# Sums of a batch placed directly behind its last weighted values, the later tails in two parts, and the root table loaded first, in a perceiver block

## The chip, the core and the metric

The kernel runs on one core of a Trainium2 chip. A core has five engines that work through queues of their own, each in order: TensorE (PE in the profile; its weight loads are listed as PEld), VectorE (DVE), ScalarE (ACT), GpSimd (POOL) and SyncE (SP, which here only starts DMA transfers). They meet through semaphores. The metric is the device time of one execution in microseconds (us), from a median of several runs.

## The reference

A block of a perceiver: 8 batches of 64 queries of width 512 look at a context of 8 x 1601 x 512, then at themselves, and then go through a mixture of experts. All is in float32. Cut to what matters:

```python
def stablemax(x):
    s = jnp.where(x >= 0, x + 1.0, 1.0 / (1.0 - x))
    return s / jnp.sum(s, axis=-1, keepdims=True)

# cross attention: 16 heads of 32, over 1601 rows of context for each batch
q, k, v = layernorm(x) @ Wq.T + bq, ctx @ Wk.T + bk, ctx @ Wv.T + bv
attn = stablemax(q k^T / sqrt(32));  x = x + (attn @ v) @ Wo.T + bo
# causal attention among the 64 queries: 8 heads of 64 that share one k and one v
y = layernorm(x);  wei = softmax(causal(q k^T * 512**-0.5));  x = x + (wei @ v) @ Wp + bp
# feed-forward: the mean of 2 shared experts, and the best 2 of 8 experts for each row
y = layernorm(x);  gates = y @ rW + rb
x = x + mean_s(gelu(y @ sW1 + sb1) @ sW2 + sb2) + sum_top2(p * (gelu(y @ W1 + b1) @ W2 + b2))
```

The denominator of stablemax is a sum over all 1601 rows of context, so the division can be done once for each batch, on the result of `attn @ v`.

## The kernel before

**How the order is made.** Nearly all the work up to the routed experts is written down in a `Plan` (L50). `plan.add(length, fn)` lays units of TensorE work one behind the other and advances the planned clock by `length`; `plan.at(time, fn)` puts other work at a planned time. `emit` then calls all of it in order of planned time, and that is the order of the program. The planned times decide nothing but the order: a scheduler lays the calls into the queues of the five engines, and on the chip each engine goes on when its semaphores allow. PSUM has seven banks that all stages share (pool `ps_a`) and one for the weighted values (`ps_o`).

**Keys and values of the context.** Each batch has three sections of 512 rows of context and a tail of 65 (1601 = 3 x 512 + 65). Tails of four batches are done together: 64 rows of each as one half-size section, and the 65th rows of all batches as `odd_rows` (L507). `products` (its products are at L376) makes keys (`ps_k`) or values (`ps_v`) of a section from seven half-size products in the manner of Strassen, a *unit* each: VectorE joins two of them to what is there (L405), ACT copies the rest (helper at L87), and POOL makes the sums of the inputs (`context_part`, L365). Sums of weights are made by VectorE (L353). A unit of a section counts `PROD` in the plan, one of a tail half of it. Tails of batches 0 to 3 are made at the start, those of batches 4 to 7 (`tail_products(1)`, 7 units of keys and 7 of values with `last`, which writes the values to DRAM, L559) behind the last section of batch 4, since `NQB` is 4. `load_vt` (L570) reads them back for each batch.

**Cross attention.** Beside those products, in units of two 128-row tiles of context (the last unit of a batch is the tail alone): `score` (L631, `ps_s`), `convert` (ACT twice relu and once +1, VectorE's reciprocal at L649, POOL's additions at L650 and, for the denominators, L662) and `weigh` (L681, `ps_o`, summed over the batch). `when` holds the planned times of the scores and `weighed` those of the weighing. When a batch is through, `sums` (L702) multiplies its totals by ones into `ps_sum`; ACT copies them to `rec`, and VectorE takes the reciprocal (L709). `finish` (L716, L717; POOL) multiplies `o_sb` by `rec` and adds the bias: that is `ctT`.

**The chain.** For every two batches (a *tile* of 128 rows, four in all) `chain` lists steps with planned gaps: project (L738, `ps_wo`), factors and apply of the layernorm, turn (L324, transposes `pt`), keys (L775, `ps_akv`), queries (L788, `ps_aq`), scores, exps, flip (L833, `pt_s`), values (L844), output (L860, `ps_ap`), and the second layernorm with its transposes and gates (`factors`, `apply2`, `rows`, `gate`). A step of the last tile is 3.2 behind the one before or less; its TensorE neighbours are no longer sections but the first shared expert's hidden layer for two thirds of its size (`first_hidden`, L1099) and second layer (`first_second`, L1111), and then `SharedHalves`, which is built of the same seven units (`ps_hh`, `ps_hr`, also L376), its start (`xt`, L935) and its gelu (L947).

**The start.** The lines of constants: `eps_t`, `one_t` and `ones` are set by VectorE, and nine products of `ones` by `ones` into `ps_one` (L246) follow, whose result nobody reads. Then come the keys of the first section done plainly (`first_keys`, L465), `odd_rows`, `odd_turn` (L525: transposes the odd rows' keys; four ACT activations add the bias into `odd_k`), the first tails and the first layernorm (`first_rows`). `ln_rs`, the root of the variance, needs ACT's table for Sqrt.

The places that count for the order, as they stand before:

```python
weighed = [t + (n + 1.5) * step for t, n in zip(when, wide)]
weighed[-1] = when[-1] + 11.0
...
        done = weighed[last]
        more = 2.0 if b < B - 1 else 0.0
        plan.at(min(when[last] + 2.4 * step, done) + more, lambda b=b: sums(b))
        plan.at(done + 1.0 + 1.5 * more, lambda b=b: finish(b))
    ...
    time = done + 1.0
    for fn, wide in steps:
        time += gap * (wide if tt < NTT - 1 else min(wide, 1))
```

Of the kernel before, what the change touches and what calls it, by code (L numbers as in the profile page):

```python
# [10 lines left out]
F32 = mybir.dt.float32  # L11
U32 = mybir.dt.uint32
I32 = mybir.dt.int32
AF = mybir.ActivationFunctionType
ALU = mybir.AluOpType
# [3 lines left out]
P = 128  # L19
B, SQ, E = 8, 64, 512  # L20
SKV = 1601
NT = B * SQ
NTT = NT // P
NC = E // P
H1, HD1 = 16, 32
NG = H1 // 4
# [12 lines left out]
NSEC = SKV // SEC  # L39
# [56 lines left out]
def perceiver_kernel(  # L96
# [7 lines left out]
    nc = tc.nc  # L104

    act = InOrder(tc, nc.scalar)

    def pool(name, bufs, **kw):
        return ctx.enter_context(tc.tile_pool(name=name, bufs=bufs, **kw))

    const = pool("const", 1)
# [29 lines left out]
    def psa(name):  # L141
        return ps_a.tile([P, 512], F32, tag="a", name=name)
# [38 lines left out]
    NQB = B // 2  # L181
# [36 lines left out]
    bk_t = bias_cols(bk, NC, "bk_t")  # L218
# [17 lines left out]
    make_identity(nc, ident)  # L236
    eps_t = const.tile([P, 1], F32, name="eps_t")
    nc.vector.memset(eps_t, EPS)
    one_t = const.tile([P, 1], F32, name="one_t")
    nc.vector.memset(one_t, 1.0)  # L240
    ones = const.tile([P, P], F32, name="ones")
    nc.vector.memset(ones, 1.0)

    ps = psa("ps_one")
    for _ in range(9):
        nc.tensor.matmul(ps[:, :P], ones, ones, start=True, stop=True)  # L246

    qT = big.tile([P, NG, NT], F32, name="qT")
# [81 lines left out]
    plan = Plan()  # L330
# [3 lines left out]
    PROD = FULL / 2  # L334
# [155 lines left out]
    odd_k = const.tile([P, NG, B], F32, name="odd_k")  # L490
# [31 lines left out]
    def odd_turn():  # L522
        pt = psa("pt_odd")[:, : NG * B].rearrange("p (g b) -> p g b", g=NG)
        for g in range(NG):
            nc.tensor.transpose(  # L525
                pt[:, g, :], odd_rows.keys[0:B, g * P : (g + 1) * P], ident[0:B, 0:B]
            )
        for g in range(NG):
            act.activation(odd_k[:, g, :], pt[:, g, :], AF.Identity, bias=bk_t[:, g : g + 1])

    def tail_parts(h):
        p = tparts["t", h]
# [3 lines left out]
    def tail_products(h):  # L536
        def keys():
            kT = tlp.tile([P, NG, NQB, TAIL], F32, name="kTt", bufs=1)
            tails["odd", h] = kT[:, :, :, ROUND:TAIL].rearrange("p g b o -> p g (b o)")
            for k in range(NQB):  # L540
                tails[h * NQB + k, "k"] = kT[:, :, k, :]
            return kT

        def values():
            v = tails["v", h] = at4("vh").rearrange("p (k e) -> p k e", k=2)
            return v

        ku = products(
            ("t", h), True, dst=keys, hf=P,
            fit=lambda ps: ps.rearrange("p k (b s) -> p k b s", s=ROUND),  # L550
        )
        vu = products(("t", h), False, dst=values, hf=P)

        def last():
            vu[-1]()
            nc.gpsimd.tensor_copy(tails.pop(("odd", h)), odd_k[:, :, h * NQB : (h + 1) * NQB])
            v = tails.pop(("v", h))
            for k in range(NQB):
                nc.sync.dma_start(  # L559
                    out=vt_d[h * NQB + k, 0:ROUND, :],  # L560
                    in_=v[(k % 2) * ROUND : (k % 2 + 1) * ROUND, k // 2, :],
                )

        if h:
            return ku + vu[:-1] + [last]
        return ku[:2] + vu[:2] + ku[2:] + vu[2:-1] + [last]

    def load_vt(b):
# [127 lines left out]
    def sums(b):  # L696


        ps = psx("ps_sum")[:, : 4 * SQ]
        a = totals.pop(b)  # L700
        for j in range(4):
            nc.tensor.matmul(  # L702
                ps[32 * j : 32 * j + 32], ones[:, 0:32], a[:, j // 2, j % 2, :],
                start=True, stop=True, skip_group_check=True,
            )
        recs[b] = accp.tile([P, NG, SQ], F32, name="rec")

        act.copy(recs[b], ps.rearrange("p (g q) -> p g q", g=NG))
        sums.last = nc.vector.reciprocal(recs[b], recs[b])  # L709

    def finish(b):
        rec = recs.pop(b)
        if b % 2 == 0:
            ctT[b // 2] = sd("ctT")
        dst = cols(ctT[b // 2])[:, :, (b % 2) * SQ : (b % 2 + 1) * SQ]
        nc.gpsimd.tensor_mul(rec, accs.pop(b), rec)  # L716
        nc.gpsimd.tensor_tensor(  # L717
            dst, rec, bv_t.rearrange("p (g o) -> p g o", o=1).to_broadcast([P, NG, SQ]), ALU.add,
        )
# [404 lines left out]
    for i, (b, k) in enumerate(secs):  # L1124
        if i == 0:
            plan.add(4 * FULL, first_keys)
            there[i] = plan.now


            def early():  # L1130
                tail_parts(0)
                wkp.update(weight_parts(wk, "sk"))
                wvp.update(weight_parts(wv, "sv"))
                early.done = weight_parts.last
                weigh_bq()

            def sums_q():
                with tc.issue_after(Norm.last.ins):
                    wqp.update(weight_parts(wq, "sq"))

            plan.at(0.05, early)
            plan.add(2.0, odd_rows)
            for k, u in enumerate(tail_products(0)):
                if k == 2:
                    plan.add(0.3, odd_turn)
                plan.add(PROD / 2, u)
            for tt in range(NTT):
                plan.add(0.5, lambda tt=tt: first_rows(tt, early.done))
            plan.at(plan.now, sums_q)
            for n in range(4):  # L1150
                plan.at(plan.now + 0.01 * n, lambda n=n: context_part("q", n))
            tparts[0] = right_parts(cxs[0])
            values0 = products(0, False)
            for u in values0[:2]:
                plan.add(PROD, u)
            for u in products("q", True, wqp, qT, Q_SCALE, bqs_t):
                plan.add(PROD, u)
            asked = plan.now
            for n in range(4):
                plan.at(asked - 9.0 + 1.5 * n, lambda n=n: context_part(0, n))  # L1160
            for u in values0[2:]:
                plan.add(PROD, u)
            for tt in range(NTT):
                plan.at(plan.now + 4.0 * tt, lambda tt=tt: add_bo(tt))
            plan.add(0.0, act.bind)
        else:
            for u in products(i, True):
                plan.add(PROD, u)
            there[i] = plan.now
            for u in products(i, False):  # L1170
                plan.add(PROD, u)

        last = len(plan.units)
        if i + 1 < len(secs):
            start = plan.now - 14 * PROD
            if i == 0:
                plan.at(0.1, lambda: load_cx(1))
                for n in range(4):
                    plan.at(plan.now - 8.0 + 2.0 * n, lambda n=n: context_part(1, n))
            else:  # L1180
                plan.at(start + 0.1, lambda i=i: load_cx(i + 1))
                for n in range(4):
                    plan.at(plan.now - (6.5 - 1.5 * n) * PROD, lambda i=i, n=n: context_part(i + 1, n))
        if k == NSEC - 1:
            if b == NQB:
                plan.at(plan.now - 30.0, lambda: load_tails(1))
                plan.at(plan.now - 15.0, lambda: tail_parts(1))
                for u in tail_products(1):
                    plan.add(PROD / 2, u)
    end = plan.now  # L1190
    step = (end - 14.0) / len(tiles_in)
    units = [(b, u) for b in range(B) for u in range(len(UNITS))]
    nu = len(UNITS)
# [7 lines left out]
    when = [max(lag + n * step, asked + 1.0 + 0.8 * n * step) for n in place]  # L1201


    wide = [len(UNITS[u]) for _, u in units]
    weighed = [t + (n + 1.5) * step for t, n in zip(when, wide)]
    weighed[-1] = when[-1] + 11.0

    pairs = [0 < u < nu - 1 and u % 2 == 1 for _, u in units]
    for u, second in enumerate(pairs):
# [16 lines left out]
    for tt in range(NTT):  # L1226
        gap = 5.0 if tt < NTT - 1 else 3.2
        for bb in range(2):
            b = 2 * tt + bb
            last = (b + 1) * nu - 1  # L1230
            done = weighed[last]

            more = 2.0 if b < B - 1 else 0.0
            plan.at(min(when[last] + 2.4 * step, done) + more, lambda b=b: sums(b))
            plan.at(done + 1.0 + 1.5 * more, lambda b=b: finish(b))
        pre, steps = chain(tt)
        for fn in pre:
            plan.at(done - 10.0, fn)
        time = done + 1.0
        for fn, wide in steps:  # L1240

            time += gap * (wide if tt < NTT - 1 else min(wide, 1))
            if fn in asks and tt < NTT - 1:

                time = min(t for t in when if t >= time - 8.0) + 6.0
            plan.at(time, fn)
# [560 lines left out]
```

## Time and profile before

| what | value |
|---|---|
| median of 3 runs | 1356.39 us (1356.39 to 1356.93) |
| the profiled execution, its own time | 1357.59 us |
| its span, first to last instruction | 1355.9 us |
| mean granted TensorE clock | 0.998 |

Busy time of the engines by stage, in us, from the profile's windows:

| stage (us of the span) | PE | DVE | ACT | POOL | DMA share |
|---|---|---|---|---|---|
| 0 to 30: first keys, odd rows, first tails | 27.8 | 10.1 | 11.0 | 12.9 | 0.84 |
| 30 to 460: cross attention, first half | 428.7 | 387.4 | 279.5 | 375.8 | 0.18 |
| 460 to 880: cross attention, second half | 417.7 | 387.9 | 268.0 | 341.9 | 0.23 |
| 880 to 960: the last tile's chain | 77.4 | 62.5 | 32.3 | 3.3 | 0.53 |
| 960 to 1000: shared experts | 39.5 | 31.1 | 11.3 | 10.8 | 0.66 |
| 1000 to 1356: shared and routed experts | 349.1 | 91.9 | 72.4 | 19.7 | 0.61 |

A span is the time from the first to the last instruction of the profiled execution; its own time is a little longer. Busy time says how full an engine is, not whether anything waits for it. In the timelines, a line is a run of equal instructions with the start of the first, the time that they cover and their number; what stands in brackets is idle time in front of it and what ended it. L numbers are lines of the kernel before.

### The profile page before, as it was taken

What the parts mean: (1) busy time and instruction counts of PE and PEld (TensorE: products, weight loads), DVE (VectorE), ACT (ScalarE), POOL (GpSimd) and SP (SyncE); (2) the same over time, 40 slices, a digit from 0 to 9 for tenths busy, and PEclk for the clock granted to TensorE, in tenths of its full rate; (3) what the DMA queues carried; (4) which work ended last, traced back from release to release, by engine and by line L of the source; (5) the groups of instructions that cost most, each with busy time, mean ns of one, the idle gap of its engine ahead of it and who ended that gap; (6) DMA issues with size and microseconds to landing.
All of it is one profiled execution on the core that took longest, in us unless ns stands there. A gap on an engine that the chain in (4) does not pass through costs nothing.

```text
span 1355.9 us, 37790 instructions
## 1 busy us (share of the span) xinstructions
PE 1340.1 (99%) x16590; PEld 1121.9 (83%) x16590; DVE 971.0 (72%) x868; ACT 674.6 (50%) x1432; POOL 764.3 (56%) x686
## 2 busy tenths in 40 slices
PE   9999999999999999999999999999999999999997
PEld 6888888888788888878888877588898999977786
DVE  3499999998999997999998999887876200010314
ACT  4466666665666665766666667335222211122230
POOL 3789899888978986988889877600200000000020
PEclk9999999999999999999999999999999999999999
DMA  7211111122402122112113114436645936788721
GB/s 212 79 41 33 37 33 64 37 79 65 157 2 72 49 75 82 47 33 64 41 46 101 65 33 164 141 126 241 220 170 173 340 129 255 266 308 325 273 89 33
DMA packets 88280, 162.76 MB, mean 120 GB/s; under 512 B 13494, under 2 KB 15062, under 8 KB 88112
## 3 DMA queue, kind: packets, MB, share of 16 engines
q1 hardware_dynamic: 81232, 142.70, 31.1%
q0 software_dynamic: 4512, 13.92, 2.9%
q10 hardware_dynamic: 2368, 3.69, 0.9%
q8 instruction: 132, 2.16, 0.7%
q14 instruction: 36, 0.29, 0.1%
HBM read 148.50 MB, written 11.78 MB: 118 GB/s over the span
## 4 chain that ended last, share of the span: by engine, by line
PE 93%; DVE 3%; ACT 2%; POOL 1%; issue 1%; DVEq 0%; POOLq 0%; ACTq 0%
PE ps_k L376 22%; PE ps_v L376 21%; PE ps_h L1640 9%; PE ps_hh L376 7%; PE ps_hr L376 6%; PE ps_s L631 5%; PE y L1552 4%; PE y L1561 4%; PE ps_o L681 3%; PE ps_h L1099 2%; DVE neg L649 1%; PE y L1111 1%; PE ps_aq L788 1%; PE ps_k L465 1%; PE ps_wo L738 1%; PE ps_ap L860 1%
## 5 line engine op out<-in xcount | busy, mean ns | idle before, releaser
L649 DVE RECIPROCAL neg<-neg 128x512 f32<-128x512 f32 (+1 forms) x224 | 686.4, 3095 | 49.9 <-ACT neg L87 48.0
L650 POOL TENSOR_TENSOR at<-at,neg 128x512 f32<-128x512 f32 (+1 forms) x224 | 269.0, 1207 | 94.3 <-DVE neg L649 80.4
L662 POOL TENSOR_TENSOR tot<-tot,at 128x512 f32<-128x512 f32 (+1 forms) x176 | 224.9, 1278 | 13.1
L87 ACT ACTIVATE neg<-neg,one_t 128x512 f32<-128x512 f32 (+1 forms) x224 | 157.7, 704 | 0.0
L87 ACT ACTIVATE neg<-ps_s 128x512 f32<-128x512 f32 (+1 forms) x224 | 127.9, 571 | 56.9 <-PE ps_s L631 50.0
L1640 PEld LDWEIGHTS ps_h<-xgT,w1t 128*128 128x128 f32 x896 | 123.0, 191 | 27.8 <-issue 26.1
L87 ACT ACTIVATE at<-ps_s 128x512 f32<-128x512 f32 (+1 forms) x224 | 128.5, 573 | 23.5 <-PE ps_o L681 23.5
L1645 ACT ACTIVATE hT<-ps_h,b1e 128x128 f32<-128x128 f32 (+3 forms) x112 | 42.7, 381 | 194.8 <-PE ps_h L1640 194.8
L376 PE MATMUL ps_v<-sv,tx 128*128 128x256 f32 x576 | 132.5, 382 | 0.0
L1640 PE MATMUL ps_h<-xgT,w1t 128*128 128x128 f32 (+3 forms) x896 | 129.2, 287 | 0.0
L1543 POOL DMA_DIRECT2D ys_d<-yo x10 | 5.4, 544 | 219.6 <-DVE yo L1542 219.6
L376 PE MATMUL ps_k<-tx,sk 128*128 128x256 f32 x552 | 128.5, 384 | 0.6 <-DVE kT L405 0.6
L376 PEld LDWEIGHTS ps_v<-sv,tx 128*128 128x128 f32 x576 | 107.7, 190 | 17.6 <-issue 1.9
L376 PEld LDWEIGHTS ps_k<-tx,sk 128*128 128x128 f32 x552 | 102.7, 190 | 16.4 <-DVE kT L405 0.7
L87 ACT COPY v<-ps_v 128x512 f32<-128x512 f32 x96 | 56.6, 589 | 78.0 <-PE ps_v L376 77.9
L1534 DVE COPY xgT<-pt_x 128x512 f32<-128x512 f32 (+3 forms) x12 | 6.8, 593 | 119.4 <-PE pt_x L1533 119.4
L87 ACT ACTIVATE kT<-ps_k,bk_t 128x256 f32<-128x256 f32 (+1 forms) x142 | 60.9, 482 | 61.4 <-PE ps_k L376 54.9
L376 PE MATMUL ps_v<-wv,cx 128*128 128x256 f32 x384 | 89.4, 382 | 0.0
L376 PE MATMUL ps_k<-cx,wk 128*128 128x256 f32 x368 | 86.5, 383 | 0.0
L631 PEld LDWEIGHTS ps_s<-qT,kT 32*64 32x64 f32 x6144 | 70.4, 130 | 16.6 <-issue 14.4
L376 PEld LDWEIGHTS ps_v<-wv,cx 128*128 128x128 f32 x384 | 71.8, 190 | 10.8 <-issue 0.4
L631 PE MATMUL ps_s<-qT,kT 32*64 32x64 f32 x6144 | 77.4, 231 | 0.4 <-DVE v L405 0.4
(303 smaller groups left out, 2242.3 us busy)
## 6 DMA issues: line engine op xcount, KB each, us to landing
w1t<-in_W_dram SPq DMA_DIRECT2D x32, 1024.0 KB, 11.0
w2t<-in_W_dram SPq DMA_DIRECT2D x32, 1024.0 KB, 9.7
cx<-in_ctxT_dram SPq DMA_DIRECT2D x23, 1024.0 KB, 5.3
w1t<-in_sW_dram SPq DMA_DIRECT2D x14, 1024.0 KB, 6.3
w2t<-in_sW_dram SPq DMA_DIRECT2D x14, 1024.0 KB, 5.6
wo<-in_woT_dram SPq DMA_DIRECT2D x4, 1024.0 KB, 7.3
awq<-in_aWq_dram SPq DMA_DIRECT2D x4, 1024.0 KB, 7.2
awp<-in_aWp_dram SPq DMA_DIRECT2D x4, 1024.0 KB
```

Of the source, the lines that this page charges most:

```text
L87: ins = getattr(self.engine, name)(*args, **kw)
L376: nc.tensor.matmul(ps[:, k, :], l[:, c, k * P : (k + 1) * P], r[:, c, :], start=first and k == 0 and c == 0, stop=last and c == 1, skip_gr ...
L631: nc.tensor.matmul(ps[j][h, k, g, :], kT[rows, g, h], qT[rows, g, b * SQ : (b + 1) * SQ], start=True, stop=True, skip_group_check=True,)
L649: nc.vector.reciprocal(neg, neg)
L650: nc.gpsimd.tensor_add(pos, pos, neg)
L662: nc.gpsimd.tensor_add(tot, tot, at[:, :, i])
L681: nc.tensor.matmul(accs[b][32 * j : 32 * j + 32, g, :], v[:w, (4 * g + j) * 32 : (4 * g + j + 1) * 32], at[j // 2][:w, j % 2, k, g, :], st ...
L1099: nc.tensor.matmul(ps[:, :N0], w0[0, q][:, c, r * P : (r + 1) * P], shared_x["x"][:, c, :N0], start=c == 0, stop=c == NC - 1,)
L1552: nc.tensor.matmul(self.y[k], hT[:, s : s + w], w2t, start=first, stop=last)
L1561: nc.tensor.matmul(y[d // 2][:, d % 2, :], w2t[:, d * P : (d + 1) * P], hT[:, : self.n], start=first and d % 2 == 0, stop=last, skip_group ...
L1640: nc.tensor.matmul(ph[:, : blk.n], w1t[:, c, f : f + P], blk.x[:, c, :], start=c == 0, stop=c == NC - 1,)
L1645: nc.scalar.activation(hT[:, : blk.n], ph[:, : blk.n], AF.Gelu, bias=blk.bias(hc))
```

## The change

Six edits, in four groups.

1. **The start.** A Sqrt activation of `eps_t` into a tile that nobody reads is put right behind `eps_t`, so that ACT's first table is that of the root. Seven products of ones instead of nine. In `odd_turn` one VectorE addition with the bias broadcast takes the place of four ACT activations.
2. **The sums.** For the tail unit of every batch but the last, `weighed` grows by 2.0; `sums` is planned at that same time instead of up to 2.0 behind the weighing, and `finish` 2.0 behind it (before, 4.0 behind the old time of weighing). The chains of tiles 0 to 2 count from `done` and so are planned 2.0 later.
3. **The later tails.** `tail_products(1)` returns keys and values apart. The keys stay behind the last section of batch 4; the values come behind the keys of section 15, the first of batch 5.
4. **The last tile.** Its first step, project, is planned 4.8 instead of 3.2 behind `done + 1.0`, and all its other steps move with it.

```diff
     nc.vector.memset(eps_t, EPS)
+
+    root_t = const.tile([P, 1], F32, name="root_t")
+    nc.scalar.activation(root_t, eps_t, AF.Sqrt)
...
-    for _ in range(9):
+    for _ in range(7):
         nc.tensor.matmul(ps[:, :P], ones, ones, start=True, stop=True)
...
-        for g in range(NG):
-            act.activation(odd_k[:, g, :], pt[:, g, :], AF.Identity, bias=bk_t[:, g : g + 1])
+        nc.vector.tensor_tensor(
+            odd_k, pt, bk_t.rearrange("p (g o) -> p g o", o=1).to_broadcast([P, NG, B]), ALU.add
+        )
...
         if h:
-            return ku + vu[:-1] + [last]
+            return ku, vu[:-1] + [last]
...
             there[i] = plan.now
+            if i == (NQB + 1) * NSEC:
+
+                for u in later_values:
+                    plan.add(PROD / 2, u)
             for u in products(i, False):
                 plan.add(PROD, u)
...
-                for u in tail_products(1):
+                later_keys, later_values = tail_products(1)
+                for u in later_keys:
                     plan.add(PROD / 2, u)
...
+    for u, (b, v) in enumerate(units):
+        if v == nu - 1 and b < B - 1:
+            weighed[u] += 2.0
...
-            more = 2.0 if b < B - 1 else 0.0
-            plan.at(min(when[last] + 2.4 * step, done) + more, lambda b=b: sums(b))
-            plan.at(done + 1.0 + 1.5 * more, lambda b=b: finish(b))
+            plan.at(done if b < B - 1 else min(when[last] + 2.4 * step, done), lambda b=b: sums(b))
+            plan.at(done + (2.0 if b < B - 1 else 1.0), lambda b=b: finish(b))
...
-            time += gap * (wide if tt < NTT - 1 else min(wide, 1))
+            time += gap * (wide if tt < NTT - 1 else 1.5 if fn is steps[0][0] else min(wide, 1))
```

## The prediction

> **What bounds the kernel.** I read part 1 of the page first (busy time by engine), then part 4 (the chain that ended last).
>
> ```profile
> PE 1340.1 (99%) x16590; PEld 1121.9 (83%) x16590; DVE 971.0 (72%) x868; ACT 674.6 (50%) x1432; POOL 764.3 (56%) x686
> PE 93%; DVE 3%; ACT 2%; POOL 1%; issue 1%; DVEq 0%; POOLq 0%; ACTq 0%
> ```
>
> PE is busy for 1340.1 of 1355.9 us and makes 93% of the chain. No edit here removes products that matter, so only two things can be gained: PE's idle time, and the time that busy PE loses where one kind of product follows another. Next the list of PE's waits, which names nearly all the first.
>
> ```profile
> PE ps_akv L775 <- DVE kTt L405: 1.7, 1, 1.7
> PE ps_wo L738 <- POOL ctT L717: 1.6, 1, 1.6
> ...
> PE ps_k L376 <- ACT kTt L87: 0.9, 1, 0.9
> ...
> PE pt L324 <- ACT xn L87: 0.5, 1, 0.5
> PE pt_s L833 <- DVE s_a L827: 0.5, 1, 0.5
> ```
>
> Columns: waiting product, what released it, us in all, times, longest. Each occurs once, so each has a place: 517.9, 884.3, 29.3, 940.9 and 920.3 us. For the second kind, the timeline of PE at the end of batch 0 (start, duration, with records two to a product):
>
> ```profile
> 158.40 0.65 PE L681 MATMUL ps_o<-at,vt 65*32 65x64 f32 x32
> 158.98 1.99 PE L376 MATMUL ps_k<-tx,sk 128*128 128x256 f32 x8
> 160.91 0.64 PE L702 MATMUL ps_sum<-tot,ones 128*32 128x256 f32 x8
> 161.48 1.99 PE L376 MATMUL ps_k<-tx,sk 128*128 128x256 f32 x8
> 163.40 1.59 PE L631 MATMUL ps_s<-qT,kT 32*64 32x64 f32 x128
> ```
>
> Starts matter, not durations. A unit of eight full-array records between two groups of narrow products takes 1.93 us (158.98 to 160.91). Sixteen in a row take 3.45 us in the chain of waits (63.97), so eight take 1.73. Entering and leaving narrow products costs 0.20 us each time. The narrow side pays too: ps_o of the tail lasts 0.58 us before a full product (158.40 to 158.98), but 0.47 before ps_sum in batch 3 (464.50 to 464.97).
>
> **1. Seven products of ones, the root table first, odd_k on VectorE.** Two products are four records of 0.213 us, 0.85 us. PE would then start the keys at 4.46 us; their first chunk has landed at 4.14, the second at 4.70, the third (8.66) is wanted after 9.1, so no transfer is in the way. But the trace's records of ps_k come 0.43 us apart up to 7.01 us and 0.216 after. If that moment stays, the 0.85 us are filled with real products at half speed: 0.43 us gained. The Trainium skill, "TensorE: Matmul & The Clock Gate", Part 1, speaks against shortening a warm-up: about 3.4 us of sustained activity release the clock, by windows that run freely. PE is busy from 1.30 either way, so a free window puts the change at the same 7.0 us (0.43 gained). A clock moved by its phase could cost or give some tenths. I use the row.
>
> The next wait is at 29.3 us: ACT's copy of kTt stands behind a table load of 1.28 us and four odd_k of 0.73 us together. Both go: the first load moves to the start, where ACT is idle till 10.4, and the one at 25.76 disappears; VectorE gets one small addition (priced like ln_rs there, 0.16). "ScalarE: Activation LUTs", What ACT_TABLE_LOAD costs, gives 1.28 us plus a drain of 1.38 us for a switch, 2.66 in all; here ln_rs starts at 27.05, right behind the load from 25.76, so the row's 1.28 holds. Row: 1.28 + 0.73 could cover the 0.93 us wait fully; with the rule even more so. Neither decides, since the new order puts two xn before kTt and these need VectorE: its fourth BN statistics ends at 26.15 (its x tile landed at 25.4, and the queue in front of it is unchanged), then kTt's join 0.41, reciprocals and ln_nb 0.5, then on ACT two xn 1.5 and two kTt 0.6: 29.05, where PE restarts at 29.35 now. Gain for all of part 1: **0.3 us**, between 0 and 0.43 + 0.93 = 1.4. The order of issue on ACT changes too: wv now waits for the landing at 8.66 instead of starting its issue at 4.54. Its queue is filled by wk until 9.1, so it loses about 1 us there; it landed at 18.1 and PE wants it at 19.6. No cost, 0.4 us if that cover fails.
>
> **2. Sums behind the last weighted values.** In the built order, batches 0 to 6 now run tail ps_o, ps_sum, ps_s without anything between. Before, batches 0, 1 and 2 had a full unit in the first gap (in 2 the tail was split once more), and all seven one in the second. Merging ps_o with ps_sum saves 0.20 + 0.11 = 0.31, three times; ps_sum with ps_s 0.20 + about 0.06 (unseen: ps_sum before a full product takes 0.55 to 0.57, two passes of 256 columns at least 0.43, so 0 to 0.13), seven times; the split 0.31. That is 0.93 + 1.82 + 0.31 = 3.06. Lost elsewhere: two pt_s no longer beside ps_o (0.39), two akv no longer beside scores (0.65), akv of the last tile cut in two (0.3); won: aq beside ps_o (0.3). Net seven entries fewer of 111, **2.0 us**, between 1.4 (entries alone) and 2.5. The sums keep their place in time, since the tail values move to them by up to two units; ACT's waits on at come from the products before the tail, so it doesn't wait longer, and finish stays at four units of plan time behind the old weighing. SP's order around these places is the same.
>
> **3. The later tails in two parts.** akv waits for its PSUM bank until VectorE has joined kTt. VectorE's timeline:
>
> ```profile
> 511.02 6.55 DVE L649 RECIPROCAL neg<-neg 128x512 f32<-128x512 f32 x2
> 517.49 0.36 DVE L405 TENSOR_TENSOR kTt<-ps_k,kTt 128x256 f32<-128x256 f32 x1
> ```
>
> The join stands behind two reciprocals until 517.85. After the change PE has two more tail units (1.9 us) between the scores' end at 516.1 and the first product that needs this bank, a key unit of section 15: it comes at 518.0, when the bank is free. akv's own bank then is one that ACT frees. Gain **1.7 us**, between 1.2 (PE comes 0.5 earlier relative to VectorE) and 1.9. What moves: seven value units, with two VectorE joins (0.42 each), four ACT copies, one POOL addition, and on SP four vt_d stores from 535.4 to about 548. SP now issues section 17's load before them; section 18's follows at 562, and the first vt reader comes at 573.9 while the reloaded vt lands near 553. Hidden by some 12 us; past that, each us costs one.
>
> **4. The last tile's project later.** Its wait of 1.64 us (1.8 with the turn) goes, as four ps_hh units (3.6 us) now precede it. But three of those need the sums of weights behind rec on VectorE:
>
> ```profile
> 880.38 1.75 DVE L709 RECIPROCAL rec<-rec 128x256 f32<-128x256 f32 x1 [1.67 <-ACT rec L87]
> 882.05 1.75 DVE L353 TENSOR_TENSOR sw<-w1t 128x512 f32<-128x512 f32 x2
> 883.73 1.09 DVE L353 TENSOR_TENSOR sw<-sw,w1t 128x512 f32<-128x512 f32 x1
> ```
>
> PE ends y at 882.5 and the first unit at 883.4; the next needs the sum that ends at 884.8 (1.35 us of waiting), the third a copy of its bank by ACT (0.45). So 1.8 us are waited again, and ps_wo starts at 888.05. Then ACT, in order:
>
> ```profile
> 890.24 1.28 ACT L87 ACT_TABLE_LOAD   x1
> 891.88 0.29 ACT L87 ACTIVATE ln_rs<-ln_mv,eps_t 128x1 f32<-128x1 f32 x1 [0.36 <-DVE ln_mv L304]
> 892.19 1.28 ACT L947 ACT_TABLE_LOAD   x1
> 893.49 1.28 ACT L947 ACTIVATE hq<-hq,b_t 128x128 f32<-128x128 f32 x4
> ```
>
> In the new order one hq copy for the second half stands behind these four lines. They start at 895.5 there (behind a copy at 895.1), 4.1 us together, so the copy ends at 899.95, and PE, which wants its bank at 898.6, waits 1.3; xnT_a comes 0.6 late for akv as well. Against that, the waits at pt_s and pt (0.6 each with the turn) go, since 7.9 and 8.4 us of products lie in the chains that needed 7.5 and 8.5. Net: 1.8 - 1.8 - 1.9 + 1.2 = **0.7 us lost**, between 1.5 lost and 2.9 gained.
>
> **Sum.** 0.3 + 2.0 + 1.7 - 0.7 = 3.3 us. The profiled execution took 1357.59 us for a span of 1355.9, so it would take 1354.3; against the median of 1356.39 that is **1353.1 us**. A lead of PE survives as VectorE, though 92% busy from 440 to 640, idles repeatedly for PE's scores and so follows.
>
> **The rivals.**
> - The end stage gains: scheduling hides the weights' sums, all three waits there go (1.8 + 0.6 + 0.6 = 3.0). For: each is listed once and now has products before it. Against: VectorE's queue behind rec. 0.3 + 2.0 + 1.7 + 2.9 = 6.9: 1349.5 us. Chance 0.25.
> - VectorE takes the lead back: from 540 on it gets two joins more where it is full (38.55 of 40 us in 560 to 600), the akv wait returns at the next bank, and half of part 2 goes. 0.3 + 1.0 - 0.7 = 0.6: 1355.8 us. For: the three small waits on VectorE from 607 to 664. Against: nine us of its idle time in 520 to 540. Chance 0.22.
> - Slower: ACT decides the last tile. If tables and gelus come once more before something PE needs (oT before ps_ap, 925 to 935), one more such pass of 4.1 us is on the path, and the loss of part 4 is 4.8: 1357.2 us. It decides once the slack I count there, 1.9 us between oT and ps_ap, is used up. Chance 0.08.
> - My forecast as it stands has 0.45, with its own range 1351.8 to 1354.4.
>
> **Numbers.** A change under 0.2% (2.7 us) can't be told from none. Faster than 1353.7: three quarters of 0.45 and all of the first rival, 0.59; within: the rest of the forecast, the second rival and most of the third, 0.35; slower, 0.06. The range for 8 in 10, 1349.3 to 1356.5, reaches from the first rival to past the second.
>
> **What would show it.** Right: no wait at akv of the second tile; tail ps_o, ps_sum and ps_s at consecutive starts with 0.47 and about 0.5 us; PE's restart near 29; a wait of 1.3 us at ps_hh on sw, just before ps_wo, and one on ACT's hq copy near 898. Wrong: the end stage without those waits, or new waits on VectorE between 540 and 670.

## The result, and the profile after

| | before | after |
|---|---|---|
| median of 18 runs each, side by side | 1357.01 us (1355.57 to 1358.77) | 1358.16 us (1356.84 to 1364.07) |
| ratio | | 1.0015 (95% interval 1.0009 to 1.0021) |
| the profiled execution, its own time | 1357.59 us | 1357.48 us |
| its span | 1355.9 us | 1355.9 us |

The ratio is estimated from all runs and puts the change at 0.15% slower, 2.0 us (1.2 to 2.9); the two medians alone are 1.15 us apart. The forecast was 3.3 us faster. Nine of the eighteen runs after lie from 1356.84 to 1357.83 us, the profiled one among them, and nine from 1358.49 up: what those lose, this profile cannot show. The two profiles have the same span; that is chance, and the last part of this section says why.

From the page of the kernel after, busy time by engine and the chain that ended last:

```profile
PE 1337.4 (99%) x16586; PEld 1121.1 (83%) x16586; DVE 971.9 (72%) x869; ACT 674.6 (50%) x1428; POOL 764.1 (56%) x686
PE 91%; DVE 4%; ACT 2%; POOL 1%; issue 1%; DVEq 0%; ACTq 0%; POOLq 0%
```

TensorE is 2.7 us less busy, so the joined groups and the missing products of ones do save work (0.97 us of it is the clock's, see below); it is idle for 2.7 us more. The list of its waits says where (columns as in the prediction):

```profile
PE ps_s L635 <- issue: 2.4, 2, 1.4
PE ps_hr L379 <- DVE res L1067: 2.0, 2, 1.5
PE ps_hh L379 <- ACT hq L973: 1.8, 2, 1.3
PE ps_hh L379 <- DVE sw L356: 1.4, 1, 1.4
PE ps_one L249 <- DVE ones L245: 1.3, 1, 1.3
PE ps_k L379 <- DVE kT L408: 0.6, 1, 0.6
PE ps_k L379 <- DVE v L408: 0.5, 1, 0.5
```

The waits at akv, ps_wo, kTt, pt_s and pt that headed the list before are gone or down to 0.2 us. Five new ones stand in their place: the first four lines and the last, at 563 us. The first has no releaser at all: "issue" in the middle of a group of scores.

**Lead by place.** I compared the start of the same group in both traces. TensorE leads the kernel before by 1.40 us at the odd rows (20 us), 2.69 at the first scores (55), 4.07 from 366 to 449, 2.85 at 485, 4.28 at 663, 2.50 at 679 and 2.07 at 863. The stage from the last ps_sum to ps_c then takes 77.85 us instead of 74.24, so 3.6 us are lost, and the one from ps_c to the first pt_x 59.30 instead of 60.82, so 1.5 come back.

**Two things in that profile are not the change's.** The clock record begins at 5.04 us, against 6.99 before; 1.95 us at half speed are 0.97 us of the lead of 1.40, and the remaining 0.43 are the forecast's figure for the two products. The first full-speed record moves from execution to execution: 4.20 to 6.98 us in eleven further profiles (and 10.95 in one whose start was slowed). And the stage from ps_c to pt_x took 59.3 to 61.2 us over all profiles, 59.3 also in one without the last tile's part (e2), 61.0 in one with it (e7). Take both away, and the profile after is 2.5 us longer than before, near the 2.0 us of the ratio.

### The profile page after: what moved, and what is told of

It reads as the page before. It is cut to its first block, busy times and chain, and to the rows that moved or that the text cites. A ratio compares the mean times of both kernels' runs of the same rounds, so it can differ in the third digit from the quotient of the medians.

```text
span 1355.9 us, 37771 instructions
## 1 busy us (share of the span) xinstructions
PE 1337.4 (99%) x16586; PEld 1121.1 (83%) x16586; DVE 971.9 (72%) x869; ACT 674.6 (50%) x1428; POOL 764.1 (56%) x686
## 4 chain that ended last, share of the span: by engine, by line
PE 91%; DVE 4%; ACT 2%; POOL 1%; issue 1%; DVEq 0%; ACTq 0%; POOLq 0%
PE ps_v L379 21%; PE ps_k L379 20%; PE ps_h L1653 9%; PE ps_hr L379 7%; PE ps_hh L379 7%; PE ps_s L635 5%; PE y L1565 4%; PE y L1574 4%; PE ps_o L685 3%; DVE neg L653 3%; PE ps_h L1103 2%; PE y L1115 1%; PE ps_aq L792 1%; PE ps_k L468 1%; PE ps_ap L864 1%
## 5 line engine op out<-in xcount | busy, mean ns | idle before, releaser
L635 PE MATMUL ps_s<-qT,kT 32*64 32x64 f32 x6144 | 78.3, 232 | 3.0 <-issue 2.4
```

Of the source, the lines that this page charges most:

```text
L635: nc.tensor.matmul(ps[j][h, k, g, :], kT[rows, g, h], qT[rows, g, b * SQ : (b + 1) * SQ], start=True, stop=True, skip_group_check=True,)
```

## The experiments

Twelve kernels ran. "Before" in each is the kernel before, run beside it.

### The four parts alone

```diff
 e1_start: part 1 of the change alone      e3_tails: part 3 alone
 e2_sums: part 2 alone                     e4_last_tile: part 4 alone
```

> The kernel before with the start alone changed (root table first, seven products of ones, odd_k on VectorE). In the profile after, TensorE's lead over the kernel before is 1.40 us at the odd rows and 2.69 us at the first scores, so by the reading that each part keeps its own gain, this one is 2.7 us faster (-0.20%). By the rival reading, that a point late in the kernel (near 993 us, where both profiles stand at the same time) is set by another engine, leads are given back there and this is within 1 us of before. The forecast had said 0.3 us.

Measured: 1355.61 us against 1356.70, ratio 0.9997 (0.9988 to 1.0006). Eight of the twelve runs lie from 1354.3 to 1355.8, four from 1358.5 to 1360.2. The profiled one is of the four. Its clock record begins at 6.97 us, as before, so its leads are the part's own: 0.45 us at the odd rows, 1.74 at the first scores, 1.71 at 655. Then -1.59 at 679: in 20 us it loses 3.3 us, in a place that the edit doesn't touch. TensorE's windows there, from the profile of e1 (busy time and records of each engine, then the granted clock, DMA share and GB/s):

```profile
662.33:665.74 3.41, 1.81 (x103) 1.58 (x86) 2.84 (x2) 0.87 (x2) 3.33 (x3) 1.00 0.12 41
665.74:669.15 3.41, 3.41 (x32) 2.34 (x34) 0.44 (x1) 0.00 (x0) 3.33 (x5) 0.50 0.02 5
669.15:672.56 3.41, 3.41 (x125) 3.11 (x115) 1.56 (x2) 2.61 (x5) 2.02 (x3) 1.00 0.02 5
```

TensorE stands for 1.60 us inside its scores ("issue" again), and the granted clock is 0.50 in the next 3.41 us, which costs another 1.7. The fall comes 658.77 us after the clock's first record, 193 times 3.413 us, and the other six falls in these profiles lie at whole multiples too: a fixed grid of windows whose phase differs by execution.

> The kernel before with the sums alone moved. Changes between narrow and full products fall by some seven, worth 1.4 to 2.0 us. Theory of instruction pages: TensorE's instructions come in pages of 256, a page is there 3.3 us after its forerunner is entered, and narrow groups that lie side by side (336 instructions in 2.1 us) use up a page before the next is there; then stalls of up to 1.1 us stand inside ps_s or ps_o at instruction counts that leave the same rest (193) when divided by 256, and the gain shrinks to about 0.5 us, -0.5 to +1 us in all with a wo load that now falls into a dense stretch (1.7 us). Rival: the moved sums cost nothing and the part gains its 2.0 us.

Measured: 1355.17 us, ratio 0.9990 (0.9981 to 0.9999), 1.4 us faster. In its profile the lead grows by 0.10, 0.53 and 0.75 us at the ends of batches 0 to 2 (0.2 is lost between, near 326 us), falls by 1.5 in batch 3 (a stall of 1.45 us from start to start in the scores behind ps_sum, "issue", at TensorE instruction 14273), and is 0.76 us larger at 863 us than at 55. A new wait of 0.50 us stands at 551, of scores for VectorE's s_a. The wait at akv is absent here.

> The kernel before with the later tails alone split in two. The wait of 1.7 us at akv goes: 1.7 us faster if nothing takes its place, as forecast; within 0.5 us of before if VectorE sets the pace from 520 to 670 us and a new wait of the same size stands at a later join.

Measured: 1357.62 us, ratio 1.0006 (0.9997 to 1.0015). The lead is 0.10 us at 55 and 0.16 at 863: nothing gained. From the list of waits of e3:

```profile
PE ps_akv L775 <- DVE kTt L405: 1.6, 1, 1.6
```

The wait that this part was to remove is still there. It goes with part 2, whose chains are planned 2.0 later: in e2 two more tail units and half of a third stand between the scores and akv. And e3 has the new wait at ps_k for VectorE's join of v (0.48 us, at 567), as have all five profiles with part 3 and none of the nine without.

> The kernel before with the last tile's project alone planned 4.8 instead of 3.2 behind. Forecast: 0.7 us slower (ps_hh waits 1.4 and 0.5 for weights' sums and 1.3 for ACT, pt_s and pt no longer wait). From the profile after, where two waits on VectorE's res additions (1.5 and 0.5 us) come on top and 1.5 us of waits from 976 to 985 us go: 2.1 us slower. If the loss after 880 us came from the earlier arrival of the other parts instead, 0.7 us or less.

Measured: 1360.34 us, ratio 1.0030 (1.0018 to 1.0041): 4.1 us slower. The stage from the last ps_sum to ps_c takes 77.84 us, as after (77.85), and 74.23 to 74.25 in all nine profiles with project at 3.2. So the part costs 3.6 us, and nothing of it is due to the other parts.

### The change without the last tile's part

```diff
-            time += gap * (wide if tt < NTT - 1 else 1.5 if fn is steps[0][0] else min(wide, 1))
+            time += gap * (wide if tt < NTT - 1 else min(wide, 1))
```

> The changed kernel without its last part: project of the last tile at 3.2 again. The last tile alone had cost 2.3 us in its profile (lead 0.70 at 863 us, -1.62 at 1014) and 2.1 us in the profile of the changed kernel. If the parts add up, this is 2.2 us faster than the changed kernel: about 1355.5 to 1356, 0.5 to 1 us faster than before. Rival: TensorE's arrival near 968 us decides nothing, since waits of 1.5 us from 976 to 985 us come back, and it is within 1 us of the changed kernel.

Measured: 1356.63 us against 1357.26, ratio 0.9996 (0.9987 to 1.0004); the stage is back at 74.24 us. The sign agrees with the sum of the parts, the interval leaves the size open.

### TensorE's instruction pages

The fourteen profiles of this study hold 21 "issue" stalls of 0.1 us or more inside narrow groups from 30 to 900 us. Idle time is meant; from start to start it is 0.2 us more. All 21 stand at TensorE instruction numbers that leave the same rest, 193, when divided by 256 (all that TensorE's queue executes counted from 0: products, weight loads and some 200 others, nearly all for semaphores). The trace lists a packet of 16 KB on an instruction queue for every 256 such instructions, and TensorE goes on 1.29 to 1.47 us after the end of the latest one (the stalls of before and after). The one at 465 us, from the timeline of TensorE after:

```profile
462.39 0.65 PE L685 MATMUL ps_o<-at,vt 65*32 65x64 f32 x32
462.86 0.62 PE L706 MATMUL ps_sum<-tot,ones 128*32 128x256 f32 x8
463.41 1.58 PE L635 MATMUL ps_s<-qT,kT 32*64 32x64 f32 x126
465.92 0.27 PE L635 MATMUL ps_s<-qT,kT 32*64 32x64 f32 x2 [0.94 <-issue]
466.12 1.13 PE L379 MATMUL ps_v<-sv,tx 128*128 128x256 f32 x4
```

The three groups hold 336 instructions (two for each record: product and weight load) in what would be 2.5 us. The page that is needed at 464.8 was fetched from 463.54 to 464.63. Over all pages of both traces, a packet begins 1.26 us at the median (half of them 1.0 to 2.3) after TensorE has started the 48th instruction before a page's end, brings the page after the next, and lasts about 1.0; with 1.3 to usability that is 3.3 us or more at most pages, and no two packets come closer than 3.33. "Runtime: NRT & Kernel Launch" of the Trainium skill, Instruction fetch mechanics, has the size (16 KiB, 256 instructions) and calls crossing a page mostly hidden; here it is hidden behind full products (eight records take 1.9 us for 16 instructions), and not where narrow groups lie side by side.

From this I worked out on the trace after, with its stalls taken out, what a shift of all pages would do. Two kernels shift them by tiny products and move nothing else:

```diff
     for _ in range(7):
         nc.tensor.matmul(ps[:, :P], ones, ones, start=True, stop=True)
+    for _ in range(11):   # e7; 21 in e8
+        nc.tensor.matmul(ps[0:32, 0:8], ones[0:32, 0:32], ones[0:32, 0:8], start=True, stop=True)
```

> The changed kernel with eleven tiny products (44 instructions) behind the seven of ones; nothing else moves. By the rule of pages (256 instructions; TensorE's queue runs up to 48 ahead; a page is usable 3.3 us after its forerunner is entered) worked out on the profile of the changed kernel, no page ends inside a stretch that is too short: no stall at 465, 529, 661 and 666 us, and about 3 us less stalled than in that profile. Rival (stalls come from the joined groups themselves, or from loads): the stalls stay where they are.

> The same with twenty-one tiny products (84 instructions). By the same rule two stalls of 1.1 us each, in the scores behind ps_sum of batches 5 and 6 (near 675 and 782 us), and none at 465 and 529 us: about 2 us slower than with eleven. Rival: no difference between the two.

e7, the same place:

```profile
464.12 0.65 PE L687 MATMUL ps_o<-at,vt 65*32 65x64 f32 x32
464.59 0.62 PE L708 MATMUL ps_sum<-tot,ones 128*32 128x256 f32 x8
465.14 1.59 PE L637 MATMUL ps_s<-qT,kT 32*64 32x64 f32 x128
```

e8, the scores behind ps_sum of batches 5 and 6:

```profile
680.29 1.34 PE L637 MATMUL ps_s<-qT,kT 32*64 32x64 f32 x101
682.96 0.35 PE L637 MATMUL ps_s<-qT,kT 32*64 32x64 f32 x10 [1.34 <-issue]
...
790.32 1.19 PE L637 MATMUL ps_s<-qT,kT 32*64 32x64 f32 x90
793.23 0.33 PE L637 MATMUL ps_s<-qT,kT 32*64 32x64 f32 x5 [1.72 <-issue]
```

The places came as worked out: none of the four old stalls in either, and in e8 the two large ones where they were named. The sizes did not (1.55 and 1.94 us of pitch instead of 1.1), and small ones came that the rule hadn't (0.5 us at 535, 605 and 768 in e7; 1.0 at 101 and 0.8 at 539 in e8). In all e7 stalls for 1.5 us instead of 3.4. The times missed altogether: e7 took 1361.60 us (ratio 1.0032, 1.0022 to 1.0043), e8 1366.23 (1.0058, 1.0046 to 1.0071). Both lose at the start: e7 is 1.7 us behind the changed kernel at the first scores, and in e8 the clock is granted at 10.95 us only and 4.3 us are lost. In e7 the clock also falls to 0.50 at 885.5, behind the waits at ps_hh, and in e8 at 683.4, behind its stall. So these two show the pages' places, not a price for the whole.

The stall at 663 us in e1 (and at 661 after) is another case: no joined groups, but a page whose packet came late, near the end of a 1 MB load. In e1 the packets of cx run from 659.32 to 662.83, and the page's begins at 662.64; after it is 660.17 in a load of wo that ends at 661.01, and in e10, further down, 660.71 in one that ends at 660.93. Before, it began at 657.31, ahead of the load (from 661.02). The start's edit has eight instructions less, so each page begins eight instructions later in the program. By the rule of 48 the packet of e1 should still have begun near 656, over 3 us before the load began, and in e5 it is late as well (660.44) but only 1.5 us into its load, and nothing stalls. So the load alone does not explain it; why the packet came so late stays open. e6 puts eight back (the lines of e7, with `range(2)`, on e1):

> The start alone, with two tiny products (32x32 by 8 columns, eight instructions) behind the seven of ones, so that TensorE's pages of 256 instructions begin at the same places of the program as before. Theory: the stall of 1.81 us at 663 us in the start alone is a page whose request came behind a load of 1 MB since it fell eight instructions later; with the old places it is gone, the clock doesn't fall to half behind it, and no run lies near 1359: all within 1354 to 1357, median 1.5 to 2 us faster than before. Rival: the stall belongs to the load and the scores alone; then a third of the runs stay 3.5 us longer and the profile can show the stall again.

Measured: 1356.42 us against 1357.26, ratio 0.9994 (0.9985 to 1.0003). No stall, and no run above 1358.1. That the outlying runs go was expected; the gain is half of what I wrote. Its profile shows two reasons: 0.33 us of the wait at kTt remain, and the wait of 1.65 us at akv, which is in the kernel before as well, lay wholly inside one window, and the clock was 0.50 in the next (517.7 to 521.2). In the profiles of before and e3 the same wait lay wholly inside one window too, and the clock stayed.

### Versions without parts 3 and 4

```diff
 e9_start_sums: parts 1 and 2 of the change, without 3 and 4
 e10_start_sums_unit, on e9:
-            weighed[u] += 2.0
+            weighed[u] += 1.0
 e11_start_sums_shift, on e9, behind the loop of odd_rows:
+        for _ in range(11):
+            nc.tensor.matmul(ps[0:32, 256:264], odd_x[:, 0, :], odd_x[:, 0, 0:8], ...)
```

> Start and sums together, without the later tails and the last tile's part. If the parts add up: 0.6 to 1.7 us from the start (how much of the wait at 29 us goes depends on when x lands) and 1.5 us from the sums, so 2 to 3 us faster than before (1354 to 1355 where before is 1357). By the rule of pages one stall of 1.1 us or more, in the scores behind ps_sum of batch 3 near 467 us. Rival: the parts share one gain (VectorE sets the pace), 1.5 us in all.

Measured: 1355.52 us against 1358.04, ratio 0.9984 (0.9975 to 0.9993): faster than both kernels, by 2.1 us against before. The stall is there (1.21 us, at 466).

> The same, but the tail's weighing 1.0 instead of 2.0 later in the plan, which leaves one full unit between ps_sum and the next scores in batches 0 to 6 while tail and sums stay side by side. Theory of pages: no stall in these scores in any batch (80 instructions, then a unit of 1.9 us, then 256), at the price of seven more changes between narrow and full products, 1.8 us; so within 1 us of the kernel without the unit, and with no run 3 us above the median. Rival (changes alone count): 1.8 us slower than without the unit.

Measured: 1357.13 us, ratio 0.9995 (0.9985 to 1.0005). No stall in the scores behind ps_sum, in any batch. But the late page stalls 1.6 us at 661 and the clock falls, and the runs go up to 1360.4: that half of the expectation failed. It is also 1.6 us slower than e9, where less than 1 was expected and the rival said 1.8; but its lead is 3.6 us in front of that page against e9's 3.05, so the profile puts the loss down to the page, the clock and a wait of 1.0 us for VectorE's join of v at 789, not to the changes of product.

> Start and sums together with eleven tiny products (44 instructions) behind the odd rows, at 20 us, which moves each page by 44 instructions. By the rule of pages no stall behind ps_sum is left (1.1 us without the shift); the products themselves cost 0.3 to 0.6 us. So 0.5 to 0.8 us faster than without the shift, 1353.5 where before is 1357. Rival: no gain, since the stall stays or others come.

Measured: 1356.36 us, ratio 0.9985 (0.9976 to 0.9993), the same as e9. The stall behind ps_sum is gone, the gain isn't: at 485 us TensorE now waits 0.9 us for VectorE's join of kT, as it does in e7 and e10. VectorE, behind its reciprocals, had that time in reserve only as long as TensorE stalled: e7, e8, e10 and e11, which do not stall near 466, all wait there, and after, e2, e5 and e9, which do, don't. At the first scores e11's profile is also 1.5 us behind that of e9, 0.8 of it a wait at kTt.

### Keys of the last tile earlier

```diff
-            time += gap * (wide if tt < NTT - 1 else min(wide, 1))
+            time += gap * (wide if tt < NTT - 1 else 1.5 if fn is steps[0][0]
+                           else 0.5 if fn is steps[4][0] else min(wide, 1))
```

> The kernel before with the last tile's project at 4.8, but its keys only 1.6 instead of 3.2 behind turn, so that keys, queries and all later steps lie among the same products of the second half as before. The stage from the last ps_sum to ps_c took 74.2 us in every profile with project at 3.2 and 77.85 in both with 4.8. If the unforeseen part of that loss (3.6 us against 0.7) is that the products of queries (3.9 us) no longer cover the chain gelu, ht, res for which ps_hr waits 1.5 us, then these waits on res go and the stage takes 76.9 us (76.5 to 77.3); the waits on weights' sums (1.4 and 0.5) and on hq (1.3) stay. If the loss comes from the order at project alone, it stays at 77.8.

Measured: 1363.14 us, ratio 1.0032 (1.0019 to 1.0044); the stage takes 80.01 us, against 77.85. The waits on res are gone as said, but another took their place. From its waits:

```profile
PE ps_akv L775 <- ACT xnT_a L87: 2.0, 1, 2.0
PE ps_hh L376 <- ACT hq L969: 1.8, 2, 1.3
```

Both longest ones lie within 5 us, and the clock was 0.50 from 906.3 to 909.7, 1.7 us of the 80.01. Without that it would be 78.3, no better than part 4 as it is. The keys were moved as well as the queries, so this is no test of the queries alone.

## Why the prediction was wrong, step by step

By the leads and stages in the profiles of the parts alone, part 1 gains 1.7 us before its late page, part 2 gains 0.8, part 3 nothing, and part 4 loses 3.6; the forecast had 0.3, 2.0 and 1.7 gained and 0.7 lost. The term of part 4 decides the sign.

**Part 1** (forecast 0.3, measured 1.7 in a profile with the same clock). The two products gave 0.43 to 0.45 us, as said. The step that was too small is the restart at 29: it took the landing of x as fixed (the fourth statistic's end at 26.15). That end lies between 23.68 and 26.14 us in thirteen profiles (27.93 in e8). With the old start the wait is 0.93 in all five profiles, wherever the statistics end: there it hangs on ACT's table load and odd_k. With the new one there is none in the three profiles where they end by 24.64 (nor in e8, where TensorE itself is late), and 0.33 to 0.88 in the five where they end at 25.17 or later. (The terms of the forecast's sum give 29.16, not 29.05.) What the forecast had no line for is the late page near 663 us: it and the clock take 3.3 us in the profiled run of e1, and, as e6 suggests, in the other three runs of that third.

**Part 2** (forecast 2.0, "the sums keep their place in time"). The saving came where it had been counted, but not all of it: 0.53 us in batch 1 (0.57 counted), 0.75 in batch 2 (0.88), 0.20 each in batches 4 and 5 (0.26); in batch 0 it was 0.10 instead of 0.57, since the scores, 0.5 us earlier, wait for VectorE's join of kT. The failed step is that a group of narrow products was priced by its products alone. Joined, they use up instructions faster than pages come: 1.45 us of stall in e2, and in the profile after 1.16 at 465 and 0.34 at 529, where queries stand directly before weighed values (the other 1.9 of its 3.4 us of "issue" belong to the late page at 661; before has 0.33). Averaged over all 64 positions of the pages that I tried in the rule, such stalls are 1.3 us for the order after and 0.1 for that before: an estimate from the two traces. It is not the whole gap. Without its stall, and without the akv wait (1.65) that went on top, the lead of e2 would have grown by 0.6 us, not 2.0. Of the missing 1.4, the wait for s_a at 551 is 0.5 and batch 0 another 0.5; the rest is not traced.

**Part 3** (forecast 1.7). The wait was right, its cure was put to the wrong edit: e3 keeps it, e2 loses it. I had read the two more units from the order with all edits in it, not from one with this edit alone. What part 3 does by itself could not be told from nothing. It does have a cost that was left out, 0.48 us near 563 to 568, where TensorE waits for VectorE's join of v.

**Part 4** (forecast 0.7 lost, measured 3.6): the term that decided the sign. Its counted terms were right: ps_hh waits 1.40, 0.46 and 1.34 us after (1.35, 0.45 and 1.3 in the forecast), the waits at ps_wo, pt_s and pt are gone (the 0.6 for xnT_a did not show as a wait). It left out what queries had covered. Before, and after, from TensorE's timeline:

```profile
902.25 1.89 PE L376 MATMUL ps_hr<-w2t,hq 128*128 128x256 f32 x8
904.07 3.95 PE L788 MATMUL ps_aq<-xnT_a,awq 128*64 128x64 f32 x128
```

```profile
900.79 1.89 PE L379 MATMUL ps_hr<-w2t,hq 128*128 128x256 f32 x8
904.21 0.70 PE L379 MATMUL ps_hr<-sw,ht 128*128 128x256 f32 x2 [1.53 <-DVE res L1067]
904.84 0.69 PE L779 MATMUL ps_akv<-xnT_a,awkv 128*64 128x64 f32 x16
905.46 0.70 PE L379 MATMUL ps_hr<-w2t,hq 128*128 128x256 f32 x2
906.09 0.69 PE L779 MATMUL ps_akv<-awkv,xnT_a 128*64 128x64 f32 x16
```

The second unit of ps_hr needs ACT's gelu, VectorE's eight sums of ht and hq (900.9 to 903.8) and the first unit's addition to res. Before, the 3.9 us of queries lay over that; after, queries come at 908.2 and TensorE waits 1.53, and 0.52 more at the same kind of place near 942. akv, cut in two, adds two more changes of product (0.4; the forecast had 0.3 for it, under part 2). That is 2.4 of the missing 2.9 us; the rest is not traced. In e12, where queries come back in front, the waits on res are gone, which fits that the cover was theirs; but there akv waits 2.0 us for xnT_a. My reading, which no run isolates, is that the path from project over ACT to xnT_a is late, and that each order pays for it somewhere.

**The rivals.** The slower one named the right stage and ACT, and its loss there (4.8) was nearer than the forecast's; the place it named, oT before ps_ap, was wrong. "VectorE takes the lead back" holds in part: the join at 485 in e7, e8, e10 and e11, and the one near 563 that part 3 brings, which the forecast had itself named as a sign of being wrong. (Of the three small waits that it ascribed to VectorE before the change, the one at 607 us has no releaser: it is a page's end, with the rest of 193.) "The end stage gains" was plainly wrong.

**The clock.** The forecast cited "TensorE: Matmul & The Clock Gate", Part 1, for a free-running window, and then kept 7.0 us as a fixed value. The runs agree with the page's window: half speed lasts 3.41 us at each of the seven falls, and the first grant moves over 2.8 us. Its table under "Why this matters for your kernels" warns only of gaps over about 3 us; here the clock fell behind windows in which TensorE was idle for 1.3 to 2.0 us of 3.41, seven times in six profiles, while other windows with 1.3 to 1.65 us idle did not bring it down. The measurement decides; what exactly is counted stays open.

## What to carry to other kernels

Before you lay narrow products side by side, count instructions as well as microseconds: a stretch of more than a page (256 here) in less time than a page takes to come (3.3 us) can be starved, and where it is starved depends on how many instructions the program has in front, so an edit at the start can move a stall to its middle. When a step of a chain is moved, list what its products were covering for other chains, not only what it waits for itself. And judge a part by the stage that it alone touches (74.24 against 77.85 us told more than eighteen runs), because clock phase and landing times move the whole by two microseconds from run to run.

## What was not expected of the hardware

- TensorE stalls on its own instructions: 0.2 to 1.9 us from start to start at a page's end, 3.4 us in all in the profile after; in three profiles the page's packet began only in the last quarter of a 1 MB load, and the stall was 1.6 to 1.8 us.
- A stall of 1.6 us cost 3.3 in e1, since the next 3.41 us ran at 0.50; an idle time of the same size inside one clock window did not do so in the profiles of before and e3.
